# The tail of a cross-attention, a 16-head attention and their feed-forward on one core: sums read from PSUM, turns in two banks, and two re-orderings

## The chip, the core and the metric

The kernel runs on one core of one Trainium2 chip. The metric is device time in microseconds (us) from one launch to its end, as the median of the runs. A core has TensorE (PE in the profile; PEld is its weight loads), VectorE (DVE), ScalarE (ACT), GpSimd (POOL) and SyncE (SP, which issues most of the transfers). Each engine works through its own list of instructions in order, and they meet by semaphores. Matmul results land in PSUM[...]; everything else lies in SBUF. All data here are fp32.

## What is computed

One layer of a Perceiver: 256 tokens `x` (512 wide) attend to a context of 25,088 rows, then to themselves, then pass through a mixture of experts.

```python
x = x + xattn(layernorm(x), ctx, ctx)      # q = xn Wq', k = ctx Wk', v = ctx Wv'; sigmoid(q k'/sqrt(128)) v
x = x + attn(layernorm(x))                 # 16 heads of 64, one shared k and v, causal softmax,
                                           # output product w_out, layernorm of the result
x = x + ffn(layernorm(x))                  # shared gated MLP (1024) + 64 experts (256), top 8 per token
```

The sigmoid attention has no normalisation, so `sum_k z[q,k] v[k]` is computed as `(z' ctx) Wv' + (row sums of z) bv`: first the product of the weights `z` with the raw context, summed over all 25,088 rows, then one product with `Wv`.

## The kernel before, in words

**The loop over the context** takes 66 groups of up to 384 rows. For each it turns the rows (DVE), makes keys (`pk`), scores (`pz`), the sigmoid (`zT`, ACT), and adds the product `z' ctx` to what lies in PSUM. That product is done by a fast 3x3 scheme: 15 small products p0 to p14 of sums of blocks (`S`, `T`), which accumulate in six banks, `xacc_0` to `xacc_5`, over the whole loop. Which product lies in which bank is the table `PRODUCTS`; in the last group the banks are finished in the order 0 to 5 (`LAST_ORDER`).

**After the loop** (L666) ACT copies the banks 0 to 4 whole to SBUF (`held`), one copy for each bank. DVE forms the two rows of the result `zc` by the 21 additions of the list `RESULTS` (L686): row 0 is c00, c01, c02, row 1 is c10, c11, c12. They read the copies, and bank 5 from PSUM. Then three small sums (`rsum`, L694) give the row sums of z. `turn_zc(t)` (L702, L709) turns row block t of `zc` by four PE transposes into one PSUM bank, and two ACT copies of two chunks each take it to `zcT`; `project_values` (`py`, L727) multiplies it by `Wv`. DVE adds it to x (`x1`), and takes the layernorm (`an`).

**Turns.** `transposed_tile` (L281) does the same for `an` and later `fn`: four transposes into one bank, then per chunk (or per half) an activation or copy by ACT or DVE (L289, L291, L296, L303).

**The heads** go in eight pairs e = 0 to 7, in a loop written out by hand over e = 0 to 9 in which three pairs overlap: `scored(e)` (`ps`, L956; DVE adds the causal mask and takes the maxima), `exponential(e)` (`pe`, ACT, L981), `divided(e-1)` (reciprocals on DVE, and `pe` multiplied by them on GpSimd, L993), `turned(e-2)` (`ptp`, six transposes, L1007, copied to `pT` by DVE and ACT), `weighted(e-2)` (`po`, L1027, copied whole to `oT` by ACT, L1035). The output product (`pw`, L930) has for each token block t eight matmuls (t, e), one for each pair. As `fillers` those that can be done early are put between the last pairs, two for each of e = 6, 7, 8 and three for e = 9: first one, then the turn of pair 7, then two. The list is (0,0) to (0,6), (1,0), (1,1). After the loop come (0,7), `attended(0)` and then (1,2) to (1,7). `attended(t)` (DVE and a little ACT, L258 to L273, L1077, L1083) ends in the layernorm `fn`; the turn of `fn` 0 stands ahead of (1,7).

**The feed-forward** runs the shared MLP in four parts (s0 to s3), the eight busiest experts, and seven more for few tokens. s0's first product (`ph_first`) is done by halves of the tokens, around the turn of `fn` 1 and the routing product `pl` (L1112). The down products of s1 to s3 and of seven experts use a 2x2 scheme of seven products (`seven`, L1269) that needs four sums of each one's down weights: `T_OF_SEVEN`, 128x256 each, made by GpSimd (`t_s`, `t_e`, L1255). GpSimd's queue also issues the two transfers that spread the routing weights (`weights_of_tokens`, L1154, L1155).

**What sets the order.** `in_turn` (L92) pins an instruction to its place in the program's order on its engine. What is not pinned is placed by a scheduler when the kernel is built. The sums of `T_OF_SEVEN` are not pinned, so some of them stand early: GpSimd's list has those of s1 ahead of the first division of the heads, and those of s2 around the divisions of pair 4. A PSUM tile is one bank[...].

## Time and profile before

| | us |
|---|---|
| median of 3 runs (782.43 to 783.6) | 782.78 |
| the profiled execution: its own time | 782.96 |
| its span, first to last instruction | 781.2 |
| busy: PE, DVE, ACT, POOL | 766.9, 554.8, 202.8, 183.7 |
| loop over the context: start of the span to the last `xacc` matmul | 0 to 551.0 |
| `zc`, its turns, `py`, `an` | 551.0 to 560.9 |
| heads and output product | 561 to 618 |
| feed-forward with the routing | 618 to 776 |
| mean granted PE clock | 0.998 |

A busy PE is one that has a matmul in flight. The matmuls overlap each other, so what counts for the time of PE is from the start of one to the start of the next; a wait shows as a longer distance, and the views of waits and of the timeline name what ended it. In the timeline a row is "start us, us, engine line op out<-in, size, xcount" and, in brackets, how long the engine stood idle before it and who released it. A matmul of fp32 is shown as two passes, so "x8" are four matmuls.

### The profile page before, as it was taken

Reading aid. Unit: us, or ns where it says so; the run is one execution under the profiler, and the core shown is the slowest. Engines: PE = TensorE matmul, PEld = TensorE weight load, DVE = VectorE, ACT = ScalarE, POOL = GpSimd, SP = SyncE. Lnnn points to the kernel's source line nnn. Section 1 sums busy time; section 2 is a strip of 40 time slices with the busy share of each in tenths; the row PEclk is TensorE's granted clock in tenths of the full one; section 3 lists DMA queues with packets and bytes.
Section 4 is the critical chain, followed back from the end, with each engine's and each line's share of the span. In section 5 each row is a group of like instructions: output and inputs, shape, how many; then the busy total and the mean of one; then the engine's idle time right before and its main releaser. Section 6 shows DMA issues by size and latency. Waiting matters only on the chain.

```text
span 781.2 us, 12389 instructions
## 1 busy us (share of the span) xinstructions
PE 766.9 (98%) x4068; PEld 623.7 (80%) x4068; DVE 554.8 (71%) x1638; ACT 202.8 (26%) x486; POOL 183.7 (24%) x346
## 2 busy tenths in 40 slices
PE   8999999999999999999999999999999999999997
PEld 6888888888888888888888888888675578887674
DVE  5978878888788788887887887887656564433223
ACT  4222222222222222222222222222435220110110
POOL 3222222223223222232232222322134002231200
PEclk9999999999999999999999999999999999999999
DMA  9999989997788887877877878740510044589600
GB/s 248 264 244 258 260 215 282 240 247 182 191 194 183 209 194 172 213 182 191 202 175 203 196 172 214 185 122 1 187 57 2 0 112 123 174 301 391 246 5 31
DMA packets 154902, 141.98 MB, mean 182 GB/s; under 512 B 9238, under 2 KB 114339, under 8 KB 154832
## 3 DMA queue, kind: packets, MB, share of 16 engines
q1 hardware_dynamic: 154000, 140.41, 69.8%
q8 instruction: 34, 0.56, 0.3%
q0 software_dynamic: 160, 0.20, 0.3%
q10 hardware_dynamic: 672, 0.52, 0.2%
q14 instruction: 36, 0.29, 0.1%
HBM read 140.52 MB, written 0.59 MB: 181 GB/s over the span
## 4 chain that ended last, share of the span: by engine, by line
PE 95%; DVE 2%; ACT 1%; POOL 1%; issue 0%; ACTq 0%; DVEq 0%; POOLq 0%
PE xacc L572 36%; PE pk L355 22%; PE pz L373 11%; PE ph_e L1168 7%; PE seven L1269 4%; PE ph_s L1168 3%; PE ph_few L1541 1%; PE pa L866 1%; PE pw L930 1%; PE py L727 1%; PE pi L211 1%; PE po_few L1572 1%; PE pf L1518 1%; PE pd_few L1586 1%; PE ps L956 1%; ACT pe L981 0%
## 5 line engine op out<-in xcount | busy, mean ns | idle before, releaser
L572 PE MATMUL xacc<-T,S 128*128 128x172 f32 (+2 forms) x912 | 185.5, 308 | 0.0
L355 PE MATMUL pk<-cT,wkT_sb 128*128 128x384 f32 x512 | 175.5, 486 | 0.0
L572 PEld LDWEIGHTS xacc<-T,S 128*128 128x128 f32 x912 | 152.6, 190 | 20.3
L355 PEld LDWEIGHTS pk<-cT,wkT_sb 128*128 128x128 f32 x512 | 97.1, 190 | 54.4
L539 POOL TENSOR_TENSOR T<-ctx 128x172 f32<-128x172 f32 x65 | 31.7, 488 | 385.7 <-PE xacc L572 379.6
L319 DVE STREAM_TRANSPOSE cT<-quarters 128x1536 f32<-128x1536 f32 x64 | 113.2, 1769 | 0.4 <-issue 0.4
L539 DVE TENSOR_TENSOR T<-ctx 128x172 f32<-128x172 f32 (+1 forms) x262 | 113.1, 432 | 0.0
L539 DVE TENSOR_TENSOR S<-zT 128x128 f32<-128x128 f32 x196 | 56.0, 286 | 72.6 <-ACT zT L382 72.6
L373 PE MATMUL pz<-qT,kT 128*128 128x256 f32 x392 | 106.0, 379 | 0.7 <-ACT kT L364 0.7
L382 ACT ACTIVATE zT<-pz 128x256 f32<-128x256 f32 (+1 forms) x131 | 64.2, 490 | 114.1 <-PE pz L373 114.1
L572 PE MATMUL xacc<-T,zT 128*128 128x173 f32 (+1 forms) x396 | 89.9, 308 | 0.0
L572 PE MATMUL xacc<-ctx,S 128*128 128x172 f32 x392 | 78.5, 309 | 0.0
L364 ACT ACTIVATE kT<-pk,bk 128x384 f32<-128x384 f32 (+1 forms) x66 | 38.1, 578 | 146.8 <-PE pk L355 146.8
L539 DVE TENSOR_TENSOR S<-zT,S 128x128 f32<-128x128 f32 x325 | 76.1, 283 | 0.0
L549 ACT COPY T<-ctx 128x170 f32<-128x170 f32 (+1 forms) x130 | 43.1, 333 | 125.4 <-PE xacc L572 124.0
L539 POOL TENSOR_TENSOR T<-ctx,T 128x170 f32<-128x170 f32 (+1 forms) x130 | 72.4, 574 | 2.2 <-PE xacc L572 2.2
L373 PEld LDWEIGHTS pz<-qT,kT 128*128 128x128 f32 x392 | 68.6, 190 | 4.8 <-ACT kT L364 1.3
L539 DVE TENSOR_TENSOR T<-ctx,T 128x172 f32<-128x172 f32 x195 | 65.6, 362 | 8.2 <-PE xacc L572 1.5
L572 PEld LDWEIGHTS xacc<-T,zT 128*128 128x128 f32 x396 | 66.4, 190 | 0.1
L572 PEld LDWEIGHTS xacc<-ctx,S 128*128 128x128 f32 x392 | 62.8, 190 | 0.0
L572 PE MATMUL xacc<-ctx,zT 128*128 128x170 f32 (+1 forms) x264 | 59.5, 307 | 0.0
L1168 PE MATMUL ph_e<-fT,gu 128*128 128x256 f32 x256 | 57.7, 381 | 0.3 <-DVE rank L1474 0.3
(274 smaller groups left out, 767.3 us busy)
## 6 DMA issues: line engine op xcount, KB each, us to landing
ctx<-in_context SPq DMA_DIRECT2D x65, 768.0 KB, 5.5
quarters<-in_context SPq DMA_DIRECT2D x256, 192.0 KB, 6.6
gu<-in_e_gate_up SPq DMA_DIRECT2D x12, 1024.0 KB, 9.0
dn<-in_e_down SPq DMA_DIRECT2D x11, 512.0 KB, 7.3
gu_s<-in_s_gate_up SPq DMA_DIRECT2D x8, 512.0 KB, 5.8
a_wqT<-in_a_wqT SPq DMA_DIRECT2D x1, 2048.0 KB, 15.9
a_wout<-in_a_woutT SPq DMA_DIRECT2D x1, 2048.0 KB, 12.8
dn_s<-in_s_down SPq DMA_DIRECT2D x4, 512.0 KB, 7.5
```

What stands on the lines that cost most here:

```text
L211: nc.tensor.matmul(pi, lhsT=idle_sb[:, 0:P], rhs=idle_sb, start=True, stop=True)
L319: in_turn(nc.vector.transpose(new_turned(g), q.rearrange("p b (c r) -> p c b r", r=R)))
L355: nc.tensor.matmul(pk, lhsT=w[:, c, :], rhs=cT[:, c, 0 : n // R, :].rearrange("p b r -> p (b r)"), start=(c == 0), stop=(c == ND - 1),)
L364: in_turn(nc.scalar.activation(kT[:, 0:n], pk, AF.Identity, bias=bk_sb))
L373: nc.tensor.matmul(pz[:, i * T : (i + 1) * T], lhsT=kT[:, at : at + P], rhs=qT, start=True, stop=True,)
L382: nc.scalar.activation(zT[:, blocks[0] : blocks[-1] + 1, :].rearrange("p j t -> p (j t)"), pz[:, 0 : len(blocks) * T], AF.Sigmoid, scale=1 ...
L539: in_turn(f(o_, a_, b_))
L549: in_turn(nc.scalar.copy(named[to][:, 0:n], named[x_][:, 0:n]))
L572: nc.tensor.matmul(banks_of_products[i][:, cols], lhsT=named[lhs], rhs=named[rhs][:, 0:n],  start=i not in opened, stop=(g == G - 1 and last),
L727: nc.tensor.matmul(pys[t], lhsT=zcT[:, c, t * P : (t + 1) * P], rhs=wvT_sb[:, c, :], start=(c == 0), stop=(c == ND - 1),)
L1168: nc.tensor.matmul(ph[:, f * T + lo : f * T + hi], lhsT=gu[:, c, col : col + P], rhs=fT[:, c, lo:hi], start=(c == 0), stop=(c == ND - 1),)
L1269: nc.tensor.matmul(product_of_seven(nm), lhsT=block(n, hT, dn, s_, t_, lhs), rhs=block(n, hT, dn, s_, t_, rhs),  start=(n == SEVEN[0] and ...
```

## The change

1. `held` shrinks to one tile of three copies by ACT: p6 (170 columns) and p14 with p8 (342 columns) of bank 0, and bank 4 whole (512). Banks 1, 2, 3 and 5 are not copied. The 21 additions are written anew so that each has one operand in PSUM at most; their number stays, the second row's order and shape are changed (`h` marks a held product).
2. `turn_zc(t)` uses two banks of two chunks each, and turn 0's first half is copied chunk by chunk. `an` 0 and `fn` 1 are turned in two banks also, the second of them `apart`.
3. The output product: the fillers become (0,0) to (0,5), (1,0), (0,6), and one instead of two is put after the turn of pair 7. So (1,0) stands ahead of that turn, (0,6) behind it, and (1,1) goes behind `attended(0)`. The last pair's `weighted` makes the two token blocks in two banks, with a copy of 128 columns for each.
4. The sums of `T_OF_SEVEN` on GpSimd are pinned. In the built program all of them now stand behind the two transfers that spread the routing weights, and each expert's go t0, t1, t2, t3 (t0, t2, t1, t3 before).

In the built program little else moves: one matmul of s1's gate product goes in between the halves of the routing product `pl` 1, and some of the routing's small DVE instructions change places. The loop over the context has the same instructions in the same order on every engine.

```diff
-        u6 p6 + p14
-        u0 p13 - p8
+        u6 p6h + p14
+        u0 p13 - p8h
...
-        u5 p3 + p13
-        u10 p3 + p5
-        u11 p12 - p0
-        u14 u11 - p6
+        u11 p12h - p0
+        u14 u11 - p6h
+        u5 p13 + p3h
         c12 u14 - u5
-        u3 p2 + p4
-        u8 p7 - p10
-        u7 p8 + u3
+        u10 p5 + p3h
+        u3 p4 + p8h
+        u7 p7 + u3
         c10 p10 + u10
-        c11 u7 + u8
+        u8 p2 + u7
+        c11 u8 - p10
     """
+    HELD = {0: (("p6", "p6"), ("p14", "p8")), 4: (("p12", "p0"),)}
...
-    for i in range(len(PRODUCTS) - 1):
-        n = max(cols.stop for b, cols in product.values() if b == i)
-        in_turn(nc.scalar.copy(held[i][:, 0:n], banks_of_products[i][:, 0:n]))
+    for n, (i, parts) in enumerate(HELD.items()):
+        for first_, last_ in parts:
+            cols = slice(product[first_][1].start, product[last_][1].stop)
+            in_turn(nc.scalar.copy(held[:, n, cols], banks_of_products[i][:, cols]))
...
-    turn_zc(0, sum_bank)
+    turn_zc(0, sum_bank, keys_bank)
...
-    turn_zc(1, sum_bank)
+    turn_zc(1, sum_bank, sum_bank)
...
-            transposed_tile(anT, an, 0, "an", ND, ln_g_sb, ln_b_sb)
+            transposed_tile(anT, an, 0, "an", ND, ln_g_sb, ln_b_sb, two=True)
...
-    fillers = [(0, e) for e in range(NE - 1)] + [(1, 0), (1, 1)]
+    fillers = [(0, e) for e in range(NE - 2)] + [(1, 0), (0, NE - 2)]
...
+        if e == NE - 1:
+            for t in range(NT):
+                po = among_three(f"po_{e}_{t}")
+                for kt in range(t + 1):
+                    for i in range(2):
+                        in_turn(
+                            nc.tensor.matmul(
+                                po[i * DH : (i + 1) * DH, 0:P],
+                                lhsT=va[:, kt, :],
+                                rhs=done[kt][:, i, (t - kt) * P : (t - kt + 1) * P],
+                                start=(kt == 0),
+                                stop=(kt == t),
+                            )
+                        )
+                in_turn(nc.scalar.copy(oT[:, e, t * P : (t + 1) * P], po[:, 0:P]))
+            return
...
-            fill(2)
+            fill(2 if e <= NE else 1)
...
-    for e in range(2, NE):
+    for e in range(1, NE):
...
-                f(*(block(n, hT, dn, s_, t_, nm) for nm in (to, x_, y_)))
+                made = f(*(block(n, hT, dn, s_, t_, nm) for nm in (to, x_, y_)))
+                if engine is nc.gpsimd:
+                    in_turn(made)
...
-    transposed_tile(fT, fn, 1, "fn", 2)
+    transposed_tile(fT, fn, 1, "fn", 2, two=True)
```

More of the change, by code (lines that the diff above doesn't have):

```diff
@@ L273, in layernorm, with transposed_tile, turned_chunk @@
         in_turn(nc.vector.tensor_scalar(dst, src, mean, rs, ALU.subtract, ALU.mult))
-    def transposed_tile(dst, src, t, nm, by_act, g=None, b=None):
+    def transposed_tile(dst, src, t, nm, by_act, g=None, b=None, two=False):
         pt = among_three(f"pt_{nm}_{t}")
+        pts = (pt, apart(f"pt_{nm}_{t}_behind")) if two else (pt, pt)
+        def turned_chunk(c):
+            return pts[c // (ND // 2)][:, c * P : (c + 1) * P]
         for c in range(ND):
-            in_turn(
-                nc.tensor.transpose(
-                    pt[:, c * P : (c + 1) * P], src[:, t, c * P : (c + 1) * P], ident
-                )
-            )
-        pc = pt.rearrange("p (c q) -> p c q", c=ND)
+            in_turn(nc.tensor.transpose(turned_chunk(c), src[:, t, c * P : (c + 1) * P], ident))
         to = dst[:, :, t * P : (t + 1) * P]
         if g is None:
-            if by_act > 0:
-                in_turn(nc.scalar.copy(to[:, 0:by_act, :], pc[:, 0:by_act, :]))
-            if by_act < ND:
-                in_turn(nc.vector.tensor_copy(to[:, by_act:ND, :], pc[:, by_act:ND, :]))
+            for lo, hi, copy in (
+                (0, by_act, nc.scalar.copy),
+                (by_act, ND, nc.vector.tensor_copy),
+            ):
+                assert not two or lo * 2 in (0, ND) and hi * 2 in (ND, 2 * ND)
+                if lo < hi:
+                    whole_bank = pts[lo // (ND // 2)].rearrange("p (c q) -> p c q", c=ND)
+                    in_turn(copy(to[:, lo:hi, :], whole_bank[:, lo:hi, :]))
             return
@@ L296, in transposed_tile @@
                     nc.scalar.activation(
-                        to[:, c, :], pc[:, c, :], AF.Identity, bias=b[:, c : c + 1],
+                        to[:, c, :], turned_chunk(c), AF.Identity, bias=b[:, c : c + 1],
                         scale=g[:, c : c + 1],
@@ L303, in transposed_tile @@
                     nc.vector.tensor_scalar(
-                        to[:, c, :], pc[:, c, :], g[:, c : c + 1], b[:, c : c + 1],
+                        to[:, c, :], turned_chunk(c), g[:, c : c + 1], b[:, c : c + 1],
                         ALU.mult, ALU.add,
@@ L463, in tile_perceiver_layer @@
         c02 p0 + u13
-        u5 p3 + p13
-        u10 p3 + p5
-        u11 p12 - p0
-        u14 u11 - p6
+        u11 p12h - p0
+        u14 u11 - p6h
+        u5 p13 + p3h
         c12 u14 - u5
-        u3 p2 + p4
-        u8 p7 - p10
-        u7 p8 + u3
+        u10 p5 + p3h
+        u3 p4 + p8h
+        u7 p7 + u3
         c10 p10 + u10
-        c11 u7 + u8
+        u8 p2 + u7
+        c11 u8 - p10
     """
+    HELD = {0: (("p6", "p6"), ("p14", "p8")), 4: (("p12", "p0"),)}
     BANK_ORDER, LAST_ORDER = (0, 1, 2, 4, 3, 5), range(6)
-    SCORE_SUMS = ("p0 + p9", "p12 - p0 + p10")
+    SCORE_SUMS = ("p0h + p9", "p12h - p0h + p10")
     WIDE = ("p2", "p4", "p7", "p8", "p9", "p10", "p11", "p13")
@@ L655, in tile_perceiver_layer @@
     zc = work.tile([P, NT, D], F32, tag="tok", name="zc")
-    held = [
-        part[:, i, :]
-        for n in range(2)
-        for part in [cpool.tile([P, J, 512], F32, tag="quarters", name=f"held_{n}", bufs=3)]
-        for i in range(J)
-    ]
+    held = cpool.tile([P, J, 512], F32, tag="quarters", name="held", bufs=3)
     u = cpool.tile([P, NU_SUMS, WIDTH], F32, tag="u", name="u", bufs=1)
     widths = {}
-    for i in range(len(PRODUCTS) - 1):
-        n = max(cols.stop for b, cols in product.values() if b == i)
-        in_turn(nc.scalar.copy(held[i][:, 0:n], banks_of_products[i][:, 0:n]))
+    for n, (i, parts) in enumerate(HELD.items()):
+        for first_, last_ in parts:
+            cols = slice(product[first_][1].start, product[last_][1].stop)
+            in_turn(nc.scalar.copy(held[:, n, cols], banks_of_products[i][:, cols]))
     def result(nm):
         if nm[0] == "p":
-            i, cols = product[nm]
-            widths[nm] = WIDTH if nm in WIDE else WIDTH - 2
-            return banks_of_products[i][:, cols] if i == len(PRODUCTS) - 1 else held[i][:, cols]
+            i, cols = product[nm.rstrip("h")]
+            widths[nm] = WIDTH if nm.rstrip("h") in WIDE else WIDTH - 2
+            if nm[-1] == "h":
+                return held[:, list(HELD).index(i), cols]
+            return banks_of_products[i][:, cols]
         if nm[0] == "c":
@@ L696, in tile_perceiver_layer, with turn_zc @@
     zcT = work.tile([P, ND, T], F32, tag="tokT", name="zcT")
-    def turn_zc(t, where):
-        pt = where(f"pt_zc_{t}")
-        for c in range(ND):
-            in_turn(
-                nc.tensor.transpose(
-                    pt[:, c * P : (c + 1) * P], zc[:, t, c * P : (c + 1) * P], ident
-                )
-            )
-        pc = pt.rearrange("p (c q) -> p c q", c=ND)
-        for c in range(0, ND, 2):
-            in_turn(
-                nc.scalar.copy(zcT[:, c : c + 2, t * P : (t + 1) * P], pc[:, c : c + 2, :])
-            )
-    turn_zc(0, sum_bank)
+    def turn_zc(t, *where):
+        for i, bank_of in enumerate(where):
+            pt = bank_of(f"pt_zc_{t}_{i}")[:, 0 : 2 * P]
+            for k in range(2):
+                c = 2 * i + k
+                in_turn(
+                    nc.tensor.transpose(
+                        pt[:, k * P : (k + 1) * P], zc[:, t, c * P : (c + 1) * P], ident
+                    )
+                )
+            pc = pt.rearrange("p (c q) -> p c q", c=2)
+            for lo, hi in ((0, 1), (1, 2)) if t == i == 0 else ((0, 2),):
+                in_turn(
+                    nc.scalar.copy(
+                        zcT[:, 2 * i + lo : 2 * i + hi, t * P : (t + 1) * P], pc[:, lo:hi, :]
+                    )
+                )
+    turn_zc(0, sum_bank, keys_bank)
     x1 = act.tile([P, NT, D], F32, tag="x1", name="x1")
@@ L1020, in weighted @@
     def weighted(e, done):
+        if e == NE - 1:
[3 more added lines that the diff above has]
+                    for i in range(2):
+                        in_turn(
+                            nc.tensor.matmul(
[4 more added lines that the diff above has]
+                                stop=(kt == t),
+                            )
+                        )
+                in_turn(nc.scalar.copy(oT[:, e, t * P : (t + 1) * P], po[:, 0:P]))
+            return
         po = among_three(f"po_{e}")
```

## The prediction

> **What bounds the kernel now.** I read the page first, then PE's waits, the chain of waits in order of time, and the timeline of the stages that the change touches.

> ```profile
> PE 766.9 (98%) x4068; PEld 623.7 (80%) x4068; DVE 554.8 (71%) x1638; ACT 202.8 (26%) x486; POOL 183.7 (24%) x346
> PE 95%; DVE 2%; ACT 1%; POOL 1%; issue 0%; ACTq 0%; DVEq 0%; POOLq 0%
> ```

> PE is the bound: 95% of the chain that ended last is PE's own work, and most of that is the loop over the context, which stays as it is. Only places where PE stands can be won. PE's waits (total, times, longest):

> ```profile
> PE ptp L1007 <- POOL pe L993: 1.8, 2, 1.5
> PE pw L930 <- ACT oT L1035: 0.9, 2, 0.5
> PE pt_fn L281 <- DVE fn L273: 0.8, 2, 0.5
> PE pt_zc L702 <- DVE zc L686: 0.7, 1, 0.7
> PE pkk L884 <- ACT anT L296: 0.5, 1, 0.5
> PE py L727 <- ACT zcT L709: 0.5, 1, 0.5
> ```

> These six make 5.2 us and lie in the stages that the change touches. They count a wait only from the end of the pipelined matmul before it; from start to start the gaps are longer, so I use starts. The longest wait, in the chain of waits (start, us, what):

> ```profile
> 591.41 0.61 POOL pe L993
> 592.02 2.05 POOL t_s L1255 x3
> 594.07 1.01 POOL pe L993
> 595.07 0.04 issue
> 595.12 0.77 PE ptp L1007 x5
> ```

> GpSimd has three sums for s2 between the two divisions of pair 4, and PE's turn waits for the second. Then the timeline after the loop, of the turn of `an`, and around the last pair:

> ```profile
> 551.49 0.33 DVE L686 TENSOR_TENSOR zc<-held,u 128x170 f32<-128x170 f32 x1
> 551.72 0.70 PE L702 MATMUL pt_zc<-ident,zc 128*128 128x128 f32 x4 [0.70 <-DVE zc L686]
> 552.45 0.65 ACT L709 COPY zcT<-pt_zc 128x256 f32<-128x256 f32 x2 [1.40 <-PE pt_zc L702]
> 552.88 1.99 PE L727 MATMUL py<-wvT,zcT 128*128 128x512 f32 x4 [0.46 <-ACT zcT L709]
> ...
> 560.93 1.51 ACT L296 ACTIVATE anT<-pt_an,ln_b,ln_g 128x128 f32<-128x128 f32 x4 [1.90 <-PE pt_an L281]
> ...
> 607.77 1.12 PE L930 MATMUL pw<-a_wout,oT 128*128 128x512 f32 x2 [0.47 <-ACT oT L1035]
> ...
> 618.47 0.63 PE L281 MATMUL pt_fn<-ident,fn 128*128 128x128 f32 x4 [0.50 <-DVE fn L273]
> ```

> The last `xacc` matmul starts at 550.71 and another could at 550.85; PE turns `zc` at 551.72 and multiplies at 552.88. At 607.77 and 612.54 it waits for copies of `oT` (0.47 each), at 618.47 for the layernorm.

> [...] the four turns of `an` start at 560.29, the first chunk is written by about 560.56, and ACT starts only at 560.93, after the fourth. [...] `u<-xacc,held` took 331 ns, `u<-held,u` 335. [...] one `t_e` sum took 1097 ns against 727.

> **1. Sums from PSUM.** From the rows: an addition follows an independent one by 0.245 us, one whose result it needs by 0.365, and takes 0.33. The copies of p6 and p14–p8 start as bank 0 does now, 547.56, and take 0.30 + 0.44 (estimates from 0.587 for 512 columns and 0.446 for 344), so u6 starts at 548.34 (now 548.18). Then u0 548.58, u1 548.95, u9 549.20, u13, u15, u2 549.94, u4 550.30, c01 550.55, c00 550.80; banks 1 to 3 are done before their readers (548.1, 549.0, 549.6). c02 waits for bank 4's copy (550.47 + 0.59): 551.09 to 551.41, against 551.81 now.
> Turn 0: chunk 0 at about 551.27, chunk 1 at 551.47 (c02), written by 551.80; ACT copies 128 columns (0.26) from 551.83, and `py` starts at 552.15, now 552.88. Row 1 runs on from c02: ten additions, three of them with a needed result just before, put c10 at 553.41 and c11 at 554.01 to 554.34. PE comes to the second half of turn 1 at 554.18 and waits for c11 until about 554.45. So of the 0.73 there stay **0.45**; this new wait is late next. Bounds: 0.2[...] and 0.7 (no wait for c11).

> **2. `an` in two banks.** ACT starts after two turns, two starts of 0.109 earlier. Its four activations of 0.35 set the pace of `pkk`, so all of it reaches PE: **0.22**. Bounds 0 and 0.25. From 561 on all is 0.67 earlier; the next times are those of the trace before, without it.

> **3. GpSimd's sums.** The division of pair 4 can start at 592.24 (its reciprocal ends 592.17) and ends at 593.28. The turn, at 593.30, goes on at once: its second transpose comes at 593.44, not 595.12, **1.67**. What is late next: scores of pair 6 start at 595.82 (597.53). The division of pair 5 hangs on ACT's exponentials, which don't move (596.41), and ends at 597.74; the turn of pair 5 waits for it by 0.15. So scores 7 start at 600.15 (601.71). From scores to the end of the division the trace has 6.27 us for pair 7 (601.71 to 607.98); 0.1 of it is DVE's queue, which goes: 606.31. The turn of pair 6 no longer waits (0.48 now), and `po` 6 starts at 604.39, not 606.43.
> The moved sums: each four cost 2.85 us on GpSimd (0.72 each, overlapping). Behind the second transfer (ends 638.59) s1's are done at 641.4; `seven` reads them at 648.97. s2's are done at 644.3 and needed after 659. In the queue both stand behind the wait for `weights_of_tokens` (1.67 us); nothing else is behind them but s3's sums, whose buffer comes free at 651. On PE they cost nothing: the cover is 7.5 us. Beside them DVE's own steps may be slowed[...]; s1's `hT` is ready at 644.6 and read at 648.1, 3.5 us of cover for some four us of DVE work. The new order t0, t1 costs the 0.08 that t1, t3 show now, once in each four.

> **4. Output product.** After `po` 6 (0.70, to 605.09) PE has (1,0), two starts of 0.43, to 605.95. Turn 7: its second transpose needs the division, 606.36, a wait of 0.3. It ends at 606.91. (0,6) follows without a wait (`oT` 6 is copied at about 605.7) and hides DVE's copy of `pT` (0.69, to 607.64): `po` at 607.77, three steps of 0.22 with the first 0.05 longer. The first block's copy of 128 columns runs beside the second block; (0,7) starts at 608.59, now 612.54, with 0.1 of wait. Its end comes 1.13 later, 609.71; the layernorm takes what it takes now (613.67 to 618.32, 4.65), to 614.36. PE has six matmuls of 0.86 after (0,7), to 614.70, so `pt_fn` 0 starts there, not at 618.47: **3.77** for parts 3 and 4, some 1.7 and 2.1. As a check: the waits removed, start to start, are 1.67, 0.48, 0.64, 0.64 and 0.67 and little ones of 0.1, together 4.2; the new ones 0.15, 0.3, 0.1. Bounds 2.6 and 4.2.

> **5. `fn` 1 in two banks.** From PE's first turn (624.79) to `ph_first` is 2.05 now. ACT's copy starts 0.22 earlier, DVE's copy no longer waits for ACT's, and the inserted gate matmul (0.43) is work moved: **0.2**, bounds 0 and 0.4. The wait before it hangs on `pw` 1 and moves along. The routing's exchanged DVE steps cost nothing: the weights' numbers are needed for transfers that land 20 us before use. In the feed-forward PE waits for the rank alone (0.3), and all of it starts earlier as it is.

> Sum: 0.45 + 0.22 + 3.77 + 0.2 = 4.64. The profiled execution took 782.96 (span 781.2 and 1.8 around it), 0.18 over the median of 782.78. 782.96 − 4.64 = 778.3; from the median 778.1. I say **778.2**.

> **Rivals.** *PSUM access eats the sums' gain* (0.13): [...] part 1 goes to nothing or below: 778.9. The equal rows for `xacc` and `held` speak against it. *The freed GpSimd isn't the limit* (0.13): if the DVE and ACT chain of pairs 5 to 7 gives back all but 0.3 of part 3, 779.6. For it: with the sums gone each pair waits a little for its division; against it: the 0.79 that GpSimd then idles ahead of pair 5. *Slower* (0.03): the pinned sums come too late for `seven`. They would have to end 4.64 after 648.97, thus start after 650.8, 12.2 later than I have them. If GpSimd's queue stood until the second transfer lands (643.9), they'd end at 646.7; every us beyond 653.6 is one lost, say 785. *The last matmuls wait for the layernorm* is no own case: it has 0.2 to spare, and each 0.1 more costs 0.1.

> **Chances.** The forecast 0.68, 777.4 to 779.0; the three rivals 0.13, 0.13, 0.03; 0.03 for better than 777.4. All the best bounds together would be 5.55 (777.4), all the worst 2.8 (780.1); with both milder rivals inside, the range is 777.4 to 779.7. A measurement tells apart about 0.2% (1.6 us): faster 0.96, same 0.02, slower 0.02.

> **What would show it.** No `t_s` before 630 on GpSimd; `pw` (0,7) ending about 4.6 earlier (0.67 of it from before 561); `py` 0.7 earlier; a wait of `pt_zc` for c11 of 0.2 to 0.3; no wait of `pw` for `oT` over 0.1; `seven` never waiting for GpSimd. Wrong if additions with `xacc` take over 0.36 us, if turn 7 waits over 0.6, or if the feed-forward grows.

## The result, and the profile after

The changed kernel took 778.72 us (median of 5 runs, 778.18 to 779.0), the kernel before beside it 782.78 (median of 5, 782.43 to 783.6): a ratio of 0.9945 [0.9931, 0.996], 4.06 us less. The profiled execution took 778.86 us (span 777.1), 4.1 less than that of before. The forecast was 778.2, from 777.4 to 779.7.

First the page after: busy times, and the engines' shares of the chain that ended last.

```profile
PE 766.2 (99%) x4072; PEld 623.7 (80%) x4072; DVE 557.9 (72%) x1638; ACT 201.4 (26%) x486; POOL 184.5 (24%) x346
PE 96%; DVE 2%; ACT 0%; DMA 0%; POOL 0%; issue 0%; ACTq 0%
```

PE does the same work (four instructions more) in 4 us less. Of its waits in the stages of the change, these are left (total, times, longest). The six shown of before made 5.2 us; the first row here was in before too, beside those six:

```profile
PE po L1055 <- ACT pT L1027: 0.4, 1, 0.4
PE pkk L895 <- ACT anT L301: 0.3, 1, 0.3
...
PE pt_fn L286 <- DVE fn L273: 0.3, 1, 0.3
```

Then the chain of waits around pairs 4 and 5 (start, us, what). Where before had 2.05 us of `t_s` sums and a division behind them, PE goes straight through the turn of pair 4 (592.50). GpSimd comes back into the chain one pair later, with the division of pair 5.

```profile
591.70 0.80 PE po L1055 x8
592.50 0.82 PE ptp L1018 x6
593.32 1.72 PE pw L941 x4
595.04 0.88 PE ps L967 x8
595.92 0.03 issue
595.94 1.05 POOL pe L1004
596.99 0.04 issue
597.04 0.76 PE ptp L1018 x5
```

The timeline after the loop, of the turn of `an`, around the last pair, and of the first turn of `fn`:

```profile
550.83 0.34 DVE L691 TENSOR_TENSOR zc<-xacc,u 128x170 f32<-128x170 f32 x1
550.91 0.86 PE L711 MATMUL pt_zc<-ident,zc 128*128 128x128 f32 x4
...
551.91 1.98 PE L738 MATMUL py<-wvT,zcT 128*128 128x512 f32 x4
...
553.73 0.93 PE L711 MATMUL pt_zc<-ident,zc 128*128 128x128 f32 x4
553.77 0.33 DVE L691 TENSOR_TENSOR zc<-u,xacc 128x172 f32<-128x172 f32 x1
...
560.07 0.81 ACT L301 ACTIVATE anT<-pt_an,ln_b,ln_g 128x128 f32<-128x128 f32 x2 [1.69 <-PE pt_an L286]
...
606.31 1.02 PE L941 MATMUL pw<-a_wout,oT 128*128 128x512 f32 x2
...
607.27 0.88 PE L1041 MATMUL po<-pT,va 128*64 128x128 f32 x12
...
608.08 6.28 PE L941 MATMUL pw<-a_wout,oT 128*128 128x512 f32 x14
...
614.19 0.60 PE L286 MATMUL pt_fn<-ident,fn 128*128 128x128 f32 x4
```

Here the last `xacc` matmul starts at 550.45 (before 550.71). `py` follows 1.45 later (before 2.17). The turn of the second row lasts 0.93, not 0.60, because c11 (553.77 to 554.10) comes late. ACT's work on `an` begins 0.42 after PE's turn does (559.65), 0.04 behind the two transposes in the first bank; before it was 0.64, 0.04 behind all four in the one bank (560.29 to 560.89, then 560.93). From (0,7) on PE goes without a gap to `pt_fn`. GpSimd's sums for s1 and s2 now lie behind the second transfer:

```profile
633.35 0.57 POOL L1183 DMA_DIRECT2D wqT<-weights_of_tokens  x1 [1.68 <-DMA weights_of_tokens<-wT]
633.94 0.74 POOL L1283 TENSOR_TENSOR t_s<-dn_s 128x256 f32<-128x256 f32 x1
...
639.52 0.77 POOL L1283 TENSOR_TENSOR t_s<-t_s,dn_s 128x256 f32<-128x256 f32 x1
```

The best measure is the time between two starts of PE: the last product of the loop and PE's last product. It was 224.31 before and 220.01 after, and a second trace of the changed kernel repeats it to 0.01. So 4.29 were won there. The rest of the span differs from trace to trace: the loop ended between 550.3 and 551.0 in twelve traces, and from PE's last start to the end it was 5.8 to 6.7. In this pair of traces the first gave 0.25 and the second took 0.45. The last of the writes of the output landed 3.7 us after its issue, in before 3.3; the last figure of each row:

```profile
DMA to landing us min/median/max: 1.8/2.0/3.3
```

```profile
DMA to landing us min/median/max: 1.8/2.0/3.7
```

That is 4.29 + 0.25 − 0.45 = 4.09, the difference of the spans. The forecast of 4.64 missed the measured 4.29 on PE by 0.35. The remaining 0.2 lies ahead of and behind the stretch that was changed.

### The profile page after: what moved, and what is told of

It reads as the page before. It is cut to its first block, busy times and chain, and to the rows that moved or that the text cites. A ratio compares the mean times of both kernels' runs of the same rounds, so it can differ in the third digit from the quotient of the medians.

```text
span 777.1 us, 12400 instructions
## 1 busy us (share of the span) xinstructions
PE 766.2 (99%) x4072; PEld 623.7 (80%) x4072; DVE 557.9 (72%) x1638; ACT 201.4 (26%) x486; POOL 184.5 (24%) x346
## 4 chain that ended last, share of the span: by engine, by line
PE 96%; DVE 2%; ACT 0%; DMA 0%; POOL 0%; issue 0%; ACTq 0%
PE xacc L579 37%; PE pk L360 22%; PE pz L378 11%; PE ph_e L1196 7%; PE seven L1299 4%; PE ph_s L1196 3%; PE pw L941 2%; PE pa L877 2%; PE ph_few L1571 1%; PE ps L967 1%; PE ptp L1018 1%; PE po_few L1602 1%; PE pf L1548 1%; PE py L738 1%; PE pd_few L1616 1%; DMA x_sb<-in_x 0%
```

## The experiments

All times are medians beside before on the same chip. For where the time went, the table gives what each kernel won against before (in us, from one trace each) between two starts of PE: (a) last `xacc` to first `pt_an`, (b) to the first `pkk`, (c) first `ps` to last `po`, (d) to `pt_fn` 0, (e) to the first product by seven; and the sum from the last `xacc` to PE's last product.

| kernel | us (runs) | before | a | b | c | d | e | sum |
|---|---|---|---|---|---|---|---|---|
| after, first | 778.72 (5) | 782.78 | 0.39 | 0.22 | 3.07 | 0.35 | 0.26 | 4.29 |
| after, again | 779.13 (5) | 783.26 | 0.39 | 0.22 | 3.07 | 0.35 | 0.27 | 4.30 |
| part 3 alone | 781.03 (10) | 783.03 | 0 | 0 | 1.65 | 0 | 0 | 1.66 |
| part 4 alone | 781.07 (10) | 783.03 | 0 | 0 | 1.41 | 0.35 | 0.03 | 1.80 |
| part 1 alone | 783.02 (13) | 783.03 | 0.38 | 0 | −0.07 | 0 | 0 | 0.32 |
| parts 2, 5 alone | 782.08 (21) | 783.03 | 0 | 0.22 | 0.27 | 0 | 0.24 | 0.73 |
| after without part 3 | 780.66 (7) | 783.26 | 0.39 | 0.22 | −0.37 | 0.35 | 0.26 | 0.85 |
| after, second row reordered | 778.32 (5) | 783.26 | 0.72 | 0.22 | 3.07 | 0.35 | 0.26 | 4.63 |
| after, division 7 on DVE | 778.35 (5) | 783.26 | 0.39 | 0.22 | 3.28 | 0.35 | 0.26 | 4.50 |
| both of these | 778.0 (5) | 783.25 | 0.72 | 0.22 | 3.29 | 0.35 | 0.26 | 4.84 |
| parts 1, 3 | 780.79 (9) | 783.25 | 0.39 | 0 | 1.91 | 0 | 0 | 2.29 |

**Part 3 alone.** The edit to before:

```
-                f(*(block(n, hT, dn, s_, t_, nm) for nm in (to, x_, y_)))
+                made = f(*(block(n, hT, dn, s_, t_, nm) for nm in (to, x_, y_)))
+                if engine is nc.gpsimd:
+                    in_turn(made)
```

> Before with part 3 alone (GpSimd's sums pinned behind the attention). My theory: GpSimd's queue is what holds the turn of pair 4, and most of it reaches the end: the second transpose of pair 4 comes 1.6 us earlier, the turn of pair 6 loses its wait of 0.48, the turn of pair 5 gains one of about 0.27 (the division starts 0.14 after its reciprocal). Sum 1.8: 781.0 against 782.8. Rival, the freed GpSimd isn't the limit: DVE's and ACT's chain of pairs 5 to 7 gives back all but 0.3, 782.5. Rival, sums late for the product by seven: slower than 782.8.

Measured: 781.03, ratio 0.9976 [0.9967, 0.9985]; in the trace 1.66. The freed GpSimd was a limit: the rival with 0.3 falls. Nothing came late for the product by seven, which was reached 1.65 sooner as well.

**Part 4 alone.** To before come the fillers, the last pair's `po` in two blocks, and the order of the second row's products:

```
-    fillers = [(0, e) for e in range(NE - 1)] + [(1, 0), (1, 1)]
+    fillers = [(0, e) for e in range(NE - 2)] + [(1, 0), (0, NE - 2)]
...
-            fill(2)
+            fill(2 if e <= NE else 1)
```

> Before with part 4 alone (the order of the output's products, the last pair's product in two blocks). My theory: it takes the two waits for oT (0.64 each, start to start) and the wait of the first fn turn (0.67), and gives back 0.1 to 0.4 in the turn of the last pair: 1.6, 781.2 against 782.8; the wait for GpSimd's second division of pair 4 stays. Rival, part 4 brings it all: 3 or more, 779.8. Rival, it needs the pinned sums before it (the waits only move to the last pair): under 0.8, 782.0 or more.

Measured: 781.07, ratio 0.9977 [0.9968, 0.9987]; in the trace 1.80. It neither brings all nor needs the pinned sums. With them it makes 3.07 in column c, about as the two alone (1.65 + 1.41).

**Part 1 alone.** To before come the sums' operands from PSUM, with only bank 0 (in two pieces) and bank 4 copied, the second row's new order, and the turn of `zc` in two banks.

> Before with part 1 alone (sums that read PSUM, zc turned in two banks). My theory: 0.39, as in the trace after (0.72 won up to py, 0.3 given back in a wait for c11): 782.4 against 782.8, the addition with xacc at 0.33 us as before. Rival, the access to PSUM eats the gain: 782.8, additions at 0.36 or more.

Measured: 783.02, ratio 1.0003 [0.9995, 1.0011]. Up to `pt_an` the trace shows the 0.38 expected, and the additions with `xacc` took 0.32 to 0.34 us, so PSUM access isn't what eats it. Two other things hide it. The first is a stall of DVE at pair 4:

```profile
591.36 0.17 DVE L998 RECIPROCAL rsm<-sums 128x2 f32<-128x2 f32 x1 [0.78 <-ACT pe L987]
591.67 0.61 POOL L999 TENSOR_TENSOR pe<-pe,rsm 128x256 f32<-128x256 f32 x1 [2.59 <-PE pa L872]
...
594.29 1.03 POOL L999 TENSOR_TENSOR pe<-pe,rsm 128x512 f32<-128x512 f32 x1
```

The first reciprocal of pair 4 waits 0.78, against 0.42 in before, though its input is ready as early. The first division, the three sums behind it and the second division all come 0.35 later. PE's stand at the turn of pair 4 (the time in which it starts nothing) grows from 1.82 us (593.30 to 595.12 in before) to 2.17 (593.21 to 595.38). Of these 0.35 column c shows only 0.07, since 0.28 comes back at pair 6, for a reason that parts 2 and 5 alone show.

The second is the clock. Of the 13 runs, seven took 781.92 to 783.02 (median 782.39, which is 0.64 below before), and six, with a mean granted clock of 0.996 or 0.997, took 783.71 to 785.05. So most of what hides the gain in the median of all 13 is the clock; a drop of it stands in the trace of after without part 3 (half for 3.41 us).

**Parts 2 and 5 alone.** To before come the two calls with `two=True`.

> Before with parts 2 and 5 alone (the turns of an and of fn 1 in two banks). My theory: 0.22 from an, 0.3 from fn 1, 782.3 against 782.8. Rival, the turns are covered or the second bank waits for its last reader: 0.2 or less, 782.6 or more.

Measured: 782.08, ratio 0.9988 [0.9982, 0.9995]; in the trace 0.73. The expected 0.22 (b) and 0.24 (e) are there, and the rival falls. The 0.27 in column c was not expected: between two pairs no step of these parts stands. It is a stall of ACT ahead of the exponentials of pair 6. In before, then in this kernel:

```profile
600.86 0.37 ACT L981 ACTIVATE pe<-ps,nmx 128x128 f32<-128x128 f32 x1 [1.18 <-DVE nmx L970]
```

```profile
600.15 0.37 ACT L986 ACTIVATE pe<-ps,nmx 128x128 f32<-128x128 f32 x1 [0.90 <-DVE nmx L975]
```

ACT idles 1.18 there in before and 0.90 without the stall.

**After again, and after without part 3.** The first is the changed kernel unchanged. The second takes part 3 back out of it.

> The changed kernel once more, beside before on the same chip and with more runs. My theory: what is won between the last product of the loop over the context and the last product of PE is 4.3 us, as in the first trace (4.29), and start and end of the program add nothing on average: 4.3 less than before. Rival, the changed kernel's last write of the output lands later as a rule (0.45 later in the first trace): 3.9 less.

Measured: 779.13, ratio 0.9945 [0.9931, 0.9958], 4.13 less than before; 4.30 in the trace. The 4.13 lies between the two forecasts, 4.3 and 3.9, and does not decide. The end of the program was 0.26 longer than in the first trace of before. The three kernels below that build on this one gave 4.9 to 5.25 by the device's clock for 4.5 to 4.84 in the trace, more and not less, so I don't take the late write for a rule.

> After with part 3 undone (GpSimd's sums where the builder puts them). My theory, the parts add up: it loses what part 3 alone won in the trace, 1.7 us, and stands 2.6 below before. Rival, the parts cover each other: it loses under 0.5 (the order of the output hides the GpSimd's delay), or over 3 (the order needs the pinned sums).

Measured: 780.66, ratio 0.9972 [0.9961, 0.9984], in two groups again: four runs at 780.03 to 780.66 and three at 782.22 to 782.71 with a clock of 0.995 to 0.997. The first group stands some 2.9 below before, near the 2.6 expected. The trace is of the second group. Its windows of 3.41 us around the turn of pair 4 (us; busy us and instructions of PE, PE's loads, DVE, ACT, POOL; granted clock; DMA share and GB/s):

```profile
591.98:595.39 3.41, 1.57 (x13) 1.08 (x10) 1.86 (x5) 2.06 (x10) 3.14 (x5) 1.00 0.01 2
595.39:598.80 3.41, 3.41 (x8) 1.14 (x8) 0.51 (x3) 0.33 (x2) 1.61 (x2) 0.50 0.00 0
598.80:602.20 3.40, 3.40 (x25) 2.04 (x24) 2.48 (x5) 0.98 (x4) 0.00 (x0) 1.00 0.00 0
```

And its chain of waits there:

```profile
591.38 2.05 POOL t_s L1283 x3
593.44 1.01 POOL pe L1004
594.44 0.04 issue
594.49 0.77 PE ptp L1018 x5
595.25 3.16 PE pw L941 x4
598.41 1.08 PE ps L967 x8
```

PE stood for 2.17 us (592.32 to 594.49), and from 595.39 the clock was granted at half for 3.41 us. The four products of 512 columns then took 3.16 instead of 1.72, the scores behind them 1.08 instead of 0.88, together 1.64. Without that the trace would stand at about 0.85 + 1.64 = 2.49. So the parts add up, and neither form of the rival holds. The fall came behind a stand of 2.17, with 1.57 us of PE's work in the 3.41 before it.

The changes of the clock lie a whole number of 3.413 us apart in the traces: here the fall at 595.39 and the one behind PE's last work, at 776.30, are 53 of them apart (180.91); in before and in the changed kernel it is 226 of them (771.41) from the first record of the clock to the fall at the end. So I read each trace as a row of windows of that length, counted back from the fall at its end, and set PE's work in a window beside the clock granted in the next. In part 4 alone the whole stand of 1.82 (592.95 to 594.77) lies in one of them, with 1.92 of PE's work, and the clock stayed at 1.00. In part 1 alone a border cuts the stand of 2.17 (593.21 to 595.38), PE's work in the two windows is 2.33 and 2.66, and the clock of that trace stayed at 1.00 there too. Part 4 alone, then part 1 alone:

```profile
591.66:595.07 3.41, 1.92 (x20) 1.08 (x17) 2.05 (x5) 1.55 (x8) 3.41 (x6) 1.00 0.01 5
```

```profile
591.21:594.63 3.42, 2.33 (x19) 1.16 (x18) 2.22 (x6) 1.56 (x8) 2.96 (x5) 1.00 0.02 5
594.63:598.04 3.41, 2.66 (x13) 1.42 (x15) 0.82 (x3) 1.98 (x9) 2.62 (x4) 1.00 0.00 0
```

So a stand of 2.17 inside one window came with a fall, and one of 2.17 cut by a border came with none. That its place in the windows decides is my guess from these three traces; it fits a fall in only some of the runs of one kernel, but no run shifts a stand within its windows.

**The second row in another order.** The edit to after; c10 and c11 come ahead of c12, and no addition but c12 itself (which still follows its u5) needs the one just before it:

```
+        u3 p4 + p8h
+        u10 p5 + p3h
+        u7 p7 + u3
+        c10 p10 + u10
+        u8 p2 + u7
         u11 p12h - p0
+        c11 u8 - p10
         u14 u11 - p6h
-        u5 p13 + p3h
-        c12 u14 - u5
-        u10 p5 + p3h
-        u3 p4 + p8h
-        u7 p7 + u3
-        c10 p10 + u10
-        u8 p2 + u7
-        c11 u8 - p10
+        u5 p13 + p3h
+        c12 u14 - u5
```

> After with the ten sums of the second row in an order in which no addition needs the one just before it, and the thirds c10, c11 ahead of c12. My theory: c11 is done a us earlier, the wait of the second row's turn (0.3, start to start) goes and nothing takes its place: 0.3 below after. Rival, the wait is another's (the copy of the row's first part, or PE's own queue): no change.

Measured: 778.32, ratio 0.994 [0.9926, 0.9954]; 0.33 more in column a, and nothing given back. The turn lasts 0.60:

```profile
553.54 0.34 DVE L691 TENSOR_TENSOR zc<-u 128x170 f32<-128x170 f32 x1
...
553.88 0.60 PE L711 MATMUL pt_zc<-ident,zc 128*128 128x128 f32 x4
```

The last of the thirds, c12, starts at 553.54 and is done as PE comes, at 553.88.

**The last pair's second division on DVE.**

```
-        nc.gpsimd.tensor_mul(pe, pe, rs.to_broadcast([P, 2, (t + 1) * P]))
+        spread = rs.to_broadcast([P, 2, (t + 1) * P])
+        if e == NE - 1 and t == 1:
+            in_turn(nc.vector.tensor_mul(pe, pe, spread))
+        else:
+            nc.gpsimd.tensor_mul(pe, pe, spread)
```

> After with the last pair's second division on DVE in place of GpSimd. My theory: GpSimd starts 0.14 after the reciprocal and takes 1.04; DVE starts at once and takes about 0.7 (as its other additions of 512 columns), so the division is done 0.45 earlier, turn 7 loses its wait of 0.14 and the next two steps their waits of 0.1: 0.14 to 0.3 below after. Rival, DVE's copy of the turned weights or the form with a spread operand takes longer (0.9 or more): no change or slower.

Measured: 778.35, ratio 0.9939 [0.9925, 0.9952]; 0.21 more in column c.

```profile
604.59 0.17 DVE L1003 RECIPROCAL rsm<-sums 128x2 f32<-128x2 f32 x1 [0.74 <-ACT pe L992]
...
604.79 0.69 DVE L1006 TENSOR_TENSOR pe<-pe,rsm 128x512 f32<-128x512 f32 x1
...
605.73 0.82 PE L1022 MATMUL ptp<-ident,pe 128*128 128x128 f32 x6
```

DVE starts 0.03 after its reciprocal and takes 0.69. GpSimd in after started 0.14 behind it (604.48 to 604.62) and took 1.04. The turn of pair 7 lasts 0.82, not 1.02.

**Both.** The two edits together.

> After with both: the sums of the second row in the new order, and the last pair's second division on DVE. My theory: the two waits are apart (one before the attention, one at its end), so the gains in the trace add up, 0.34 and 0.21: 0.55 between the last product of the loop and PE's last product, 4.85 below before there; by the clock of the device 4.6 below before. Rival, the later wait takes back what the earlier one gives (pair 5 or 7 waits for GpSimd by so much more): 0.3.

Measured: 778.0 (777.56 to 778.74), ratio 0.9933 [0.9919, 0.9946]; in the trace 4.84. The gains add up as expected. By the trace this kernel is 0.55 shorter than the changed one; the runs of the two (778.0 beside 783.25, 779.13 beside 783.26) point the same way, though the intervals of their ratios overlap.

**Parts 1 and 3.** To before come both edits, to see what lowers the clock.

> Before with parts 1 and 3 (the sums from PSUM, and GpSimd's sums pinned). With part 1 alone, and with part 3 alone undone, PE stood 2.17 us from one transpose of pair 4 to the next (1.82 in before), and about half of the runs showed a mean clock of 0.995 to 0.997 and 1.5 to 2 us more. My theory: it is the longer stand that lowers the clock, and the pinned sums take the stand away: no run under 0.998, 0.3 + 1.7 = 2.0 to 2.3 below before. Rival, part 1 itself (the reads of PSUM) lowers the clock: about half of the runs under 0.998, at 1.5 us more than the others.

Measured: 780.79, ratio 0.9971 [0.9962, 0.9981]; all nine runs between 0.998 and 1.0. The rival falls: the reads of PSUM are in, the stand is out, and the clock stays. DVE's stall is in this trace too and costs nothing, since no sums follow the first division. Against part 3 alone, column c has 0.26 more: part 1 also takes ACT's stall away.

## Why the prediction was right, and where it was off

In the sum the terms were off by 0.06, 0, 0.35 and, the other way, 0.06; that the first and the last cancel is luck.

**1. Sums from PSUM, 0.45 forecast, 0.39 measured.** The mechanism was right: `py` 0.72 sooner (0.73 forecast), additions with `xacc` at 0.33, then a wait for c11. That wait was 0.31 (0.27 forecast), which the reordered row confirms by winning 0.33. The first rival, dearer access to PSUM, is out: the additions show it.

**2. `an` in two banks, 0.22 forecast, 0.22 measured**, alone and together.

**3 and 4. GpSimd's sums and the output's products, 3.77 forecast, 3.42 measured** (c and d). Right in kind: each part won alone what the whole takes from it, 1.66 and 1.80 where I had some 1.7 and 2.1. From the last `po` to `pt_fn` it is 6.32, as forecast (the last `po` starts 0.61 into its group). The sizes that failed lie between pair 5 and the last `po`, 0.34 in all:

- "The division of pair 5 … ends at 597.74". That lets GpSimd start 0.03 after the reciprocal, and scores 7 at 600.15 leave nothing between the division's end and PE. Measured are 0.14 (595.80 to 595.94) and 0.06 (596.98 to 597.04). Scores 7 came 0.15 later than forecast, with the shifts before them taken off. In before a first division in GpSimd's queue hid this at pair 5, but turns that nothing disturbs showed it: from the first to the second transpose pairs 1 and 3 took 0.41 (580.11 to 580.52) and 0.42 (588.80 to 589.22), as pair 5 does now (596.62 to 597.04).
- "From scores to the end of the division the trace has 6.27 us for pair 7 … 0.1 of it is DVE's queue": measured 6.21, 0.05 more than the 6.16 left.
- "It ends at 606.91": the turn of pair 7 took 0.60 from its second transpose, not 0.55; that of pair 4 in before took 0.60 as well (595.12 to 595.72). PE's wait in it was 0.14, not the 0.3 forecast, because PE itself came later.
- "(0,6) … hides DVE's copy of `pT`": not quite. The copy ends at 606.99, (0,6) lets PE go at 607.18, and `po` starts at 607.27: 0.09. What holds `po` for these 0.09 is not shown.

One step was right in its sum and wrong in its cause, so its size held by luck. "The turn of pair 6 no longer waits (0.48 now)": of this, 0.26 to 0.27 was ACT's stall. Part 3 alone keeps it; parts 2 and 5 alone take it away. It is not what GpSimd's sums cost. In the whole that stall is gone too, and yet c is 3.07 and not 3.06 + 0.26. The rest goes into the turn of the last pair: freed of both, PE reaches it before its division is done. The chain of waits has for this turn, with part 4 alone and then in the whole (start, us, what):

```profile
608.01 0.65 PE ptp L1007 x6
```

```profile
605.62 0.85 PE ptp L1018 x6
```

That is 0.20 of the 0.26, which the division on DVE wins back (0.21).

**5. `fn` 1 in two banks, 0.2 forecast, 0.26 measured** (0.24 with parts 2 and 5 alone).

The sums of GpSimd on their new place ran as forecast: s1's from 633.94 to 636.84 (641.4 forecast; 636.9 with the 4.54 taken off by which seven starts earlier), seven at 643.78 without a wait. That leaves 6.9 us, so the slower rival had no ground. The rival in which the freed GpSimd isn't the limit fell with part 3 alone. One of s2's sums took 1.27 us and not 0.72 (638.29); in that time DVE multiplied `hT_s` by `wqT` (638.30 to 638.97). Nobody waited for it.

**What stays open.** The stalls of DVE (pair 4) and ACT (pair 6) stand ahead of instructions whose inputs were ready: 0.40 from the semaphore before it to the instruction on DVE where 0.04 is usual, 0.33 on ACT where 0.05 is. ACT's is in the traces of before and of parts 3 and 4 alone, at the same place in its order, and in no other. DVE's is in every trace with part 1, but not where the second row is reordered. So in these traces they came and went with the instructions ahead of them on that engine. Why, no run here isolates. One hint stands in the profiles: the page lists a DMA queue of the kind `instruction`, q14, with pieces of 8 KB. In each of the nine traces with one of the two stalls, such a piece starts 0.64 to 0.87 us after the stalled instruction (in the changed kernel at 591.27, after 590.58). In the two traces with the second row reordered, where DVE's stall is gone, it starts ahead of pair 4, at 587.98 and 588.03. What these pieces carry, and whether they have to do with the stalls, no run tests. In the changed kernel DVE's costs next to nothing (the second division starts 0.16 after its reciprocal, elsewhere 0.14), ACT's is gone.

## What to carry to other kernels

Cost each hand-over from engine to engine between dependent instructions, also where the trace before hides it behind a queue: here the two around one division made 0.15 of the miss of 0.35, and undisturbed pairs of the trace before showed their size. Before crediting a wait to the engine named, look whether that engine had its input and idled; a stall of 0.3 can lie inside. Where PE is the bound, a stand can cost more than its length: here one of 2.17, with 1.57 of PE's work in the 3.41 us before the fall, was followed by half the clock and cost another 1.64. Work on another engine between two halves of one turn is worth moving for that alone.
